# The bias of a projection copied into its PSUM banks one item earlier

## The chip, the cores and the metric

The kernel runs on one core of one Trainium2 chip. The metric is the device time of the whole kernel in microseconds (us); smaller is better. A core has five engines that run side by side and meet through semaphores: TensorE (PE in the profile, its weight loads PEld), VectorE (DVE), ScalarE (ACT), GpSimd (POOL) and SyncE (SP), which here only issues DMA transfers. Matmuls write to PSUM[...]; ACT and DVE read them from there.

## The reference

Two graph layers with a residual and a layer norm each, on x of 16 batches x 1024 nodes x 128 features and one 1024 x 1024 matrix `adj`, all in float32:

```python
# layer 0
support = einsum('bnf,fo->bno', x, weight)
x = layernorm(x + einsum('nm,bmo->bno', adj, support) + bias)
# layer 1: five steps of a gated unit, h = x at the start
m  = einsum('nm,bmd->bnd', adj, h);  av = concat([m, m])
u3 = h @ u3_w.T + u3_b
z  = sigmoid(av @ w3_w.T + w3_b + u3);  r = sigmoid(av @ w4_w.T + w4_b + u3)
hv = tanh(av @ w5_w.T + w5_b + (r * h) @ u5_w.T + u5_b)
h  = (1 - z) * h + z * hv
x = layernorm(x + h)
```

The kernel multiplies by `adj` first and by `weight` after it, which gives the same sum for layer 0.

## The kernel before

Batches are taken four at a time (a quad; `q` counts four of them). For each quad, `aggregate` multiplies `adj` by the four batches. It doesn't do this block by block: it uses a scheme of seven products in place of eight, on two levels. On the outer level there are seven products, done in four groups, each by one call of `chain`: the groups are named 12, 3, 67 and 54. On the inner level, each chain has seven items again, taken in the order 1, 5, 6, 2, 7, 3, 4. An item is a set of matmuls (L398) into one of three PSUM banks: pa for items 1 and 2, pc for 5 and 3, pb for 6, 7 and 4. In chain 12, 67 and 54 an item has four matmuls of 256 columns, in chain 3 two. The profile lists two records for each float32 matmul.

Behind each item stands one reading of its bank: ACT copies (L382 from pa into pb after item 1, L383 after 5, L384 after 6, L385 after 2, L388 after 4) and DVE additions (L386 after 7, L387 after 3). The next item that uses the bank has to wait for that reading. So item 4 of a chain can write pb only after L386 has read item 7 there.

DVE forms the sums that the scheme needs on the way in (L317 to L320 for the inner level, L347 to L351 for the outer), and the sums on the way out (L437, L446 to L448, L455, L457), which fill the tile `agg` with the four aggregated batches.

Layer 0 is done for all four quads first, in the aggregations with the tags x0 to x3. The rest of layer 0 for the quad before, the projection, is put inside the next aggregation: `projections` (L664) hands `chain` 12 a dictionary of hooks, functions to be called ahead of an item. Batch k of the quad is projected ahead of item 5 (k = 0), 2 (k = 1), 3 (k = 2) and at the end of chain 12 (k = 3). The last quad's projections lie in the first aggregation of layer 1, tag 0_0. So there are four blocks with four projections each: in x1, x2, x3 and 0_0.

A projection (`project`) works in two PSUM banks, seeded0 and seeded1, one for each half of the 1024 nodes. For each half ACT copies the bias, broadcast to 512 columns, into the bank (L469); four chunks are added to it by matmuls of 128 columns with the weight (L472, eight matmuls or sixteen records for both halves); DVE adds the bank to the input (L477). Since there is one pair of banks, the copy of a projection must wait until L477 of the projection before has read them. Then follow the statistics of the layer norm on DVE (L256, L258), its scale and shift on POOL (L269 to L272), and its application on ACT (L275), which `drain` puts one or two at a time behind later items; at last a DMA stores the batch (L281).

Later, in layer 1, the same two banks serve the gates (L506, L531); the change doesn't touch that part.

What sets the order of instructions: the framework orders each engine's instructions by dependencies and priorities. `tc.keep_in_program_order` keeps marked instructions of an engine in the order of the code, `tc.high_priority` draws instructions ahead where they can go. The readings behind the items, the bias copies and L477 have high priority, so their places among others follow from the framework's plan, and so do the places of the matmuls between them. An engine executes its own list in order. In the compiled order of before, projection 0 lies behind the third of the four products of item 5, projection 1 behind the third of item 2, projection 2 between items 7 and 3, and projection 3 inside chain 3, between the two products of its item 5.

Of the kernel before, what the change touches and what calls it, by code (L numbers as in the profile page):

```python
# [20 lines left out]
def kernel(  # L21
# [32 lines left out]
    nc = tc.nc  # L54
    B, N, D = x.shape
    P = 128
# [4 lines left out]
    CH = C // 2  # L61
# [10 lines left out]
    rows = const.tile([P, QUAD, N], F32, name="rows")  # L72
# [16 lines left out]
    seeded = [ps_m.tile([P, HALF], F32, name=f"seeded{i}") for i in range(2)]  # L89
# [14 lines left out]
    def chunked(t):  # L104
        return t.rearrange("p (c d) -> p c d", c=C)

    def chunk_cols(t, c):

        return t.rearrange("p (n q c) -> p n c q", n=4, c=2)[:, c // 2, c % 2]
# [5 lines left out]
    def x_rows(b):  # L115
        return x[b].rearrange("(p c) d -> p (c d)", c=C)
# [10 lines left out]
    for i, c in enumerate([*range(CH), "x0", "x1", *range(CH, C), "x2", "x3"]):  # L127
        queue = queues[i % 2 if i < 6 else 0]
        if isinstance(c, str):
            k = int(c[1])  # L130
# [77 lines left out]
    b0_bc = const.tile([P, D], F32, name="b0_bc")  # L208
# [6 lines left out]
    def layer0_weights():  # L215
        nc.sync.dma_start(w0_sb, w0)
        nc.sync.dma_start(b0_bc, bass.AP(tensor=b0.tensor, offset=b0.offset, ap=[[0, P], [1, D]]))
# [114 lines left out]
    def sums_of(src, ns, pinned=False):  # L332
        t = inner[0 if ns in ((1, 2), (6, 7)) else 1]
        for op in inner_sums(blocks_of(src, ns), [t[:, i, : len(ns)] for i in range(4)]):
            if pinned:
                tc.keep_in_program_order(op)
        return op
# [16 lines left out]
    def behind_closing():  # L354

        return tc.issue_after(closed[0].ins) if closed[0] else nullcontext()
# [100 lines left out]
                nc.vector.tensor_add(agg[:, dst, :HALF], agg[:, dst, :HALF], p5[:, cols])  # L457


    def project(q, k, y):  # L460

        b = q * QUAD + k
        y = chunked(y)
        for h in range(2):
            po = seeded[h]
            po3 = po.rearrange("p (k d) -> p k d", k=CH)
            with tc.high_priority():
                tc.keep_in_program_order(
                    nc.scalar.copy(po3, b0_bc[:, None, :].broadcast_to([P, CH, D]))  # L469
                )  # L470
            for c in range(CH):
                nc.tensor.matmul(  # L472
                    po3[:, c, :], chunk_cols(agg[:, k], h * CH + c), w0_sb, start=False, stop=True,
                    skip_group_check=True,
                )
            with tc.high_priority():
                nc.vector.tensor_add(y[:, ts(h, CH), :], po3, y[:, ts(h, CH), :])  # L477
        layernorm(y, f"0_{b}", chunked(saved[b]))
# [175 lines left out]
    def call(f, *args):  # L654
        return lambda: f(*args)


    def projections(q):

        room = rooms[q % 2]  # L660
        ys = [ypad[0], ypad[1], room[:, 2], room[:, 3]]
        for k in (2, 3):
            nc.sync.dma_start(ys[k], x_rows(q * QUAD + k))
        return {a: [call(project, q, k, ys[k])] for k, a in enumerate((5, 2, 3, "end"))}  # L664

    def added_left():

# [41 lines left out]
    for q in range(NQ):  # L709
        room = rooms[q % 2]  # L710
        hooks = {}
        if q == 0:
            hooks[12] = {
                5: [turn_rest, added_sums, added_left],
                6: [outer_left, call(sums_of, rows, (3,))],
                7: [rest_sums, call(inner_left, 6), call(inner_left, 7)],
            }
            hooks[67] = {1: [call(inner_left, 5), call(inner_left, 4)]}
            layer0_weights()
            with tc.issue_after(last_left.ins):  # L720
                sums_of(rows, (1, 2))
        else:
            hooks[12] = projections(q - 1)
            hooks[12][6] = [call(sums_of, room, (3,)), call(outer_sums, room, False, True)]

        def fetch(q=q):
            drain(99, 0)
            if q == 0:

                for dst, b in [(hid[:, k], QUAD + k) for k in range(QUAD)] + [  # L730
                    (ypad[k], k) for k in range(2)
                ]:
                    tc.keep_in_program_order(nc.gpsimd.dma_start(dst, x_rows(b)))
                load_layer1_weights()
                return
            for k in range(2):
                nc.sync.dma_start(ypad[k], x_rows(q * QUAD + k))
            if q + 1 < NQ:
                load(q + 1, rooms[(q + 1) % 2], x_rows)
            else:  # L740
                load(0, rows, saved_rows)

        def ahead(room):
            sums_of(room, (1, 2))
            outer_sums(room, True, False)

        hooks.setdefault(67, {})["end"] = [fetch]
        hooks[54] = {7: [call(ahead, rooms[(q + 1) % 2])]}
        if q == 1:
            hooks[54][5] = [layer1_weights]  # L750
            hooks[54][4] = [turn_weights]
        if q == 0:
            with tc.issue_after(last_left.ins):
                aggregate(f"x{q}", room, hooks, False)
        else:
            aggregate(f"x{q}", room, hooks, False)
# [83 lines left out]
    for q in range(NQ):  # L840
        for s in range(STEPS):
            tag = f"{q}_{s}"
            if s == 0:
                if q == 0:
                    hooks = {
                        12: projections(NQ - 1),
                        3: {5: [call(to_hidden, 0)], 2: [call(to_hidden, 1)]},
                        67: {
                            3: [call(drain, 99, 0), call(to_hidden, 2)],
                            "end": [call(to_hidden, 3)],  # L850
                        },
                        54: {},
                    }
                    hooks[12][6] = [call(sums_of, rows, (3,)), call(outer_sums, rows, False, True)]
                else:
                    outer_sums(rows)
                    hooks = {54: {}}
            else:
                hooks = {54: {}}
            last = s == STEPS - 1  # L860
            end = last and q == NQ - 1

            k = s if q else s - 1
            if q < NQ - 1 and 0 <= k < QUAD:
                hooks[3] = {1: [call(next_load, q + 1, k)]}
                hooks[67] = {1: [call(next_turn, k)]}
            if q > 0 and s > 0:
                hooks.setdefault(67, {})[5] = [call(close_load, q - 1, s - 1)]
                hooks[54] = {6: [call(close, q - 1, s - 1)]}
            if q == s == 0:  # L870
                hooks[54][3, (0,)] = [call(gates_begin, tag, 3)]
            hooks[54][4] = [call(gate_r, 0, False)]
            hooks[54][3, (1,)] = [call(gate_z, 0)]
            aggregate(tag, rows, hooks, s > 0)
            if end:
                load(q, rows, saved_rows)
            elif last:
                load(q + 1, rows, saved_rows)
            with behind_closing():
                gate_rh(0)  # L880
            if not end:
                gate_seed(2)
            gate_r(1)
            gate_z(1)
            if end:
                turns[0] = part_of[2]
                ending(q, tag)
                break

            def updated(k):  # L890
                if last:
                    turn_rows(k, None, closing[k])
                    fetch_hidden(k)
                elif k < 3:
                    turn_rows(k)
                    if k < 2:
                        fetch_rows(k)

            def step_update(u, part):
                k, h = UNITS[u]  # L900
                if last and u == 4:
                    sums_of(rows, (1, 2))
                    sums_of(rows, (3,))
                update_half(tag, k, h, part, not last and k == 3)
                if u % 2:
                    updated(k)

            for u in range(3, 8):
                gate_first(tag, u, (u - 3) % 3)
                step_update(u - 3, (u - 2) % 3)  # L910
                gate_r(u - 1)
                gate_z(u - 1)
            step_update(5, 2)
            gate_r(7)
            gate_z(7)
            step_update(6, 0)
            step_update(7, 1)
            part_of.insert(0, part_of.pop())
            then = f"{q}_{s + 1}" if not last else f"{q + 1}_0"
            gates_begin(then, 2 if q == NQ - 1 and s == STEPS - 2 else 3)  # L920
            if not last:
                fetch_rows(3, 1)
                fetch_rows(3, 0)
# [32 lines left out]
```

## Time and profile before

| | us |
|---|---|
| three runs | 1771.13, 1771.18, 1771.88 |
| their median | 1771.18 |
| span of the profiled execution, first to last instruction | 1769.3 |
| PE busy in it | 1757.7 (99%) |
| DVE busy | 1302.9 (74%) |
| ACT busy | 799.2 (45%) |
| POOL busy | 103.6 (6%) |
| the four blocks in it, start of the first projected item to the last projection | 61.4 to 79.1, 112.4 to 130.1, 163.0 to 180.7, 213.7 to 231.4 |
| 32 bias copies L469 on ACT | 17.8, 0.595 each |
| 32 additions L477 on DVE | 21.5, 0.69 each |

The profile is of one execution; the page gives its span, and no device time for it. In the lists by order of time a row has its start, its length, engine, line, operation, what it writes and reads, its size, and how many instructions were drawn together (x). In brackets stands how long the engine was idle before it and what ended this. Lengths include some time in which the next instruction of the engine already runs, so the step from start to start is the better measure. The clock that TensorE was granted is 0.999 over the whole span.

### The profile page before, as it was taken

The numbers are of one execution on the slowest core, as the hardware profiler recorded it, in microseconds if no ns is written. First come the engines' busy times: TensorE is split into PE (matmuls) and PEld (weight loads), VectorE is DVE, ScalarE is ACT, GpSimd is POOL, SyncE is SP. The second block draws the span as 40 slices with busy tenths as digits, with TensorE's granted clock in tenths as the row PEclk, the third lists the DMA queues.
The fourth block names the chain that finished last, engine by engine and source line by source line (L and its number), as shares of the span: only waits on it lengthen the run. The fifth ranks groups of instructions, "written<-read, shape, count | busy, mean of one in ns | idle before, by whom it ended". The sixth has DMA issues, their size and how long they took to land.

```text
span 1769.3 us, 19948 instructions
## 1 busy us (share of the span) xinstructions
PE 1757.7 (99%) x6709; PEld 1264.5 (71%) x6709; DVE 1302.9 (74%) x2286; ACT 799.2 (45%) x1424; POOL 103.6 (6%) x152
## 2 busy tenths in 40 slices
PE   9999999999999999999999999999999999999997
PEld 8888885766758577685867758586675857668584
DVE  7977777676766857777777667777778577777778
ACT  4355555344352434435354442535445353443537
POOL 1202120000000000000000000000000000000004
PEclk9999999999999999999999999999999999999999
DMA  8144354141422505143351424324243241514232
GB/s 276 49 143 143 120 130 107 26 114 30 96 60 72 143 13 130 48 121 68 87 131 54 114 54 101 81 75 119 53 114 98 58 92 28 131 25 107 60 84 95
DMA packets 405332, 161.34 MB, mean 91 GB/s; under 512 B 388336, under 2 KB 389488, under 8 KB 405232
## 3 DMA queue, kind: packets, MB, share of 16 engines
q1 hardware_dynamic: 402960, 153.01, 34.1%
q0 software_dynamic: 1696, 5.24, 1.1%
q10 hardware_dynamic: 576, 1.84, 0.3%
q8 instruction: 53, 0.87, 0.2%
q14 instruction: 47, 0.39, 0.1%
HBM read 93.98 MB, written 65.01 MB: 90 GB/s over the span
## 4 chain that ended last, share of the span: by engine, by line
PE 98%; DMA 1%; DVE 0%; POOL 0%; ACT 0%; issue 0%; POOLq 0%; SPq 0%; DVEq 0%; ACTq 0%
PE pb L398 25%; PE pc L398 14%; PE pa L398 14%; PE pu L516 8%; PE ph L539 8%; PE ph L540 8%; PE pu L498 8%; PE seeded L531 8%; PE pc_x L398 3%; PE pa_x L398 3%; PE seeded L472 2%; DMA hid<-in_adj_dram 1%; DMA agg<-in_adj_dram 0%; PE pt L630 0%; PE pt_end L831 0%; POOL rstd L265 0%
## 5 line engine op out<-in xcount | busy, mean ns | idle before, releaser
L398 PE MATMUL pb<-e,inner 128*128 128x256 f32 x864 | 206.3, 379 | 0.2 <-ACT pb L382 0.2
L555 DVE TENSOR_TENSOR tsum<-tsum,hid 128x512 f32<-128x512 f32 x158 | 108.7, 688 | 106.4 <-ACT tsum L550 106.3
L550 ACT ACTIVATE tsum<-ph,bh 128x512 f32<-128x512 f32 x158 | 108.6, 687 | 164.3 <-PE ph L540 164.2
L398 PEld LDWEIGHTS pb<-e,inner 128*128 128x128 f32 x864 | 167.7, 194 | 19.5 <-ACT pb L382 0.9
L516 PE MATMUL pu<-agg,w_t 128*128 128x512 f32 x320 | 163.7, 593 | 0.0
L539 PE MATMUL ph<-agg,w_t 128*128 128x512 f32 x320 | 163.4, 592 | 0.0
L531 PE MATMUL seeded<-agg,w_t 128*128 128x512 f32 x320 | 163.4, 592 | 0.0
L540 PE MATMUL ph<-tsum,u_t 128*128 128x512 f32 x320 | 163.4, 592 | 0.0
L498 PE MATMUL pu<-hid,u_t 128*128 128x512 f32 x320 | 157.0, 592 | 0.0
L519 ACT ACTIVATE tsum<-pu,br 128x512 f32<-128x512 f32 x160 | 110.1, 688 | 85.5 <-PE pu L516 85.5
L398 PE MATMUL pb<-s,inner 128*128 128x256 f32 x576 | 148.4, 380 | 0.0
L398 PE MATMUL pb<-a,inner 128*128 128x256 f32 x576 | 143.9, 379 | 0.0
L526 DVE TENSOR_TENSOR tsum<-tsum,hid 128x512 f32<-128x512 f32 x160 | 110.2, 688 | 37.7 <-ACT tsum L519 37.7
L398 PE MATMUL pc<-e,inner 128*128 128x256 f32 x560 | 134.3, 379 | 0.0
L398 PEld LDWEIGHTS pb<-s,inner 128*128 128x128 f32 x576 | 110.5, 194 | 24.6 <-issue 10.2
L534 ACT ACTIVATE tsum<-seeded,bz 128x512 f32<-128x512 f32 x160 | 110.0, 688 | 29.3 <-PE seeded L531 29.3
L398 PEld LDWEIGHTS pb<-a,inner 128*128 128x128 f32 x576 | 111.9, 194 | 12.4
L398 PEld LDWEIGHTS pc<-e,inner 128*128 128x128 f32 x560 | 109.1, 195 | 12.7 <-issue 0.7
L540 PEld LDWEIGHTS ph<-tsum,u_t 128*128 128x128 f32 x320 | 60.8, 190 | 76.5 <-issue 59.1
L539 PEld LDWEIGHTS ph<-agg,w_t 128*128 128x128 f32 x320 | 60.6, 190 | 75.1 <-issue 74.4
L498 PEld LDWEIGHTS pu<-hid,u_t 128*128 128x128 f32 x320 | 60.8, 190 | 73.5 <-issue 72.2
L556 DVE TENSOR_TENSOR tsum<-tsum 128x512 f32<-128x512 f32 x158 | 109.1, 691 | 4.9
(192 smaller groups left out, 2856.3 us busy)
## 6 DMA issues: line engine op xcount, KB each, us to landing
turned<-ypad SPq DMA_DIRECT2D x48, 512.0 KB, 3.8
rows<-turned SPq DMA_DIRECT2D x192, 128.0 KB, 2.8
hvs<-saved SPq DMA_DIRECT2D x24, 512.0 KB, 4.1
rows<-saved SPq DMA_DIRECT2D x20, 512.0 KB, 3.8
hid<-hidden SPq DMA_DIRECT2D x64, 128.0 KB, 3.3
turned<-ypad SPq DMA_DIRECT2D x32, 256.0 KB, 2.9
rows<-turned SPq DMA_DIRECT2D x128, 64.0 KB, 2.1
hidden<-ypad SPq DMA_DIRECT2D x12, 512.0 KB, 4.1
```

What stands on the lines that cost most here:

```text
L398: product = nc.tensor.matmul(bank_of[a][:, ts(o, QT)], chunk(a, o, c), left[n][a][:, c, :], start=(a in (1, 5) and o == 0 and c == 0), sto ...
L498: in_order(nc.tensor.matmul(pu, w_t["u3"], hid[:, k, ts(h, HALF)], start=True, stop=True, skip_group_check=True))
L516: in_order(nc.tensor.matmul(pu, w_t["w4"], agg[:, k, cols], start=False, stop=True, skip_group_check=True))
L519: pin(nc.scalar.activation(rh[:, cols], pu, AF.Sigmoid, bias=br))
L526: pin(nc.vector.tensor_mul(rh[:, cols], rh[:, cols], hid[:, k, cols]))
L531: in_order(nc.tensor.matmul(pz, w_t["w3"], agg[:, k, cols], start=False, stop=True, skip_group_check=True))
L534: pin(nc.scalar.activation(z_of[k % 2][:, cols], pz, AF.Sigmoid, bias=bz))
L539: in_order(nc.tensor.matmul(ph, w_t["w5"], agg[:, k, cols], start=True, stop=False))
L540: in_order(nc.tensor.matmul(ph, w_t["u5"], rh_of[k % 2][:, cols], start=False, stop=True))
L550: pin(nc.scalar.activation(hv, ph, AF.Tanh, bias=bh))
L555: pinned(nc.vector.tensor_sub(hv, hv, hid[:, k, cols]))
L556: pinned(nc.vector.tensor_mul(hv, hv, z_of[k % 2][:, cols]))
```

## The change

The copies of the bias leave `project` and become a function of their own, `seed_bias`, which writes both banks. It is called by hooks one item earlier: ahead of item 1 for the projection ahead of item 5, ahead of 6 for the one ahead of 2, ahead of 7 for the one ahead of 3, and ahead of 4 for the one at the end. Where item 6 has hooks of its own, the lists are joined, with the copies first.

```diff
+    def seed_bias():
+        for po in seeded:
+            with tc.high_priority():
+                tc.keep_in_program_order(nc.scalar.copy(
+                    po.rearrange("p (k d) -> p k d", k=CH),
+                    b0_bc[:, None, :].broadcast_to([P, CH, D]),
+                ))
+
     def project(q, k, y):
...
         for h in range(2):
-            po = seeded[h]
-            po3 = po.rearrange("p (k d) -> p k d", k=CH)
-            with tc.high_priority():
-                tc.keep_in_program_order(
-                    nc.scalar.copy(po3, b0_bc[:, None, :].broadcast_to([P, CH, D]))
-                )
+            po3 = seeded[h].rearrange("p (k d) -> p k d", k=CH)
             for c in range(CH):
                 nc.tensor.matmul(
...
-        return {a: [call(project, q, k, ys[k])] for k, a in enumerate((5, 2, 3, "end"))}
+        hooks = {a: [call(project, q, k, ys[k])] for k, a in enumerate((5, 2, 3, "end"))}
+        hooks.update({a: [seed_bias] for a in (1, 6, 7, 4)})
+        return hooks
...
-            hooks[12][6] = [call(sums_of, room, (3,)), call(outer_sums, room, False, True)]
+            hooks[12][6] += [call(sums_of, room, (3,)), call(outer_sums, room, False, True)]
...
-                    hooks[12][6] = [call(sums_of, rows, (3,)), call(outer_sums, rows, False, True)]
+                    hooks[12][6] += [call(sums_of, rows, (3,)), call(outer_sums, rows, False, True)]
```

The compiled order follows suit. On ACT the copies of projection 0 come ahead of L382, those of projection 1 ahead of L384, those of projection 2 stay behind L385, those of projection 3 come ahead of L388. On TensorE each projection stands whole between two items: 0 behind item 1, 1 behind item 6, 2 behind item 7, 3 behind item 4 and ahead of chain 3. On DVE the additions L477 come some places earlier among the statistics and sums. The lists of POOL and SP are the same.

## Prediction

> **What bounds the kernel now.** I read the page first, then the view of the instructions on the projection's line L472, then TensorE's order of time around one block, then the busy time of the four blocks, and last the rows of VectorE and of TensorE's weight loads behind each block.
>
> ```profile
> span 1769.3 us, 19948 instructions
> PE 1757.7 (99%) x6709; PEld 1264.5 (71%) x6709; DVE 1302.9 (74%) x2286; ACT 799.2 (45%) x1424; POOL 103.6 (6%) x152
> PE 98%; DMA 1%; DVE 0%; POOL 0%; ACT 0%; issue 0%; POOLq 0%; SPq 0%; DVEq 0%; ACTq 0%
> ```
> ```profile
> L472 PE MATMUL seeded<-w_sb,agg x256: 272/281/386, 62.8 to 233.3; 128*128 128x128 f32 x128
> ACT seeded L469: 3.5, 12
> ```
> TensorE sets the end. The bias copies L469 hold its weight loads back 12 times, 3.5 us in all. There are 16 projections, so four don't wait.
>
> ```profile
> 61.41 1.56 PE L398 MATMUL pc_x<-e,inner 128*128 128x256 f32 x6
> 62.81 2.13 PE L472 MATMUL seeded<-w_sb,agg 128*128 128x128 f32 x16
> 64.78 0.60 PE L398 MATMUL pc_x<-e,inner 128*128 128x256 f32 x2
> 65.21 1.89 PE L398 MATMUL pb<-e,inner 128*128 128x256 f32 x8
> 66.94 1.46 PE L398 MATMUL pa_x<-a,hid 128*128 128x256 f32 x6
> 68.32 2.15 PE L472 MATMUL seeded<-w_sb,agg 128*128 128x128 f32 x16
> 70.31 0.60 PE L398 MATMUL pa_x<-a,hid 128*128 128x256 f32 x2
> 70.75 1.89 PE L398 MATMUL pb<-e,inner 128*128 128x256 f32 x8
> 72.47 2.04 PE L472 MATMUL seeded<-w_sb,agg 128*128 128x128 f32 x16
> 74.35 1.89 PE L398 MATMUL pc_x<-e,hid 128*128 128x256 f32 x8
> ```
> Read the starts, not the lengths: rows overlap. Eight 256-column records take 1.73 us (65.21 to 66.94), and sixteen of a projection that doesn't wait take 1.88 (72.47 to 74.35).
>
> ```profile
> 61.41:79.14 17.73, 17.73 (x104) 15.67 (x103) 17.21 (x64) 6.51 (x13) 6.43 (x8) 1.00 0.29 90
> 112.37:130.09 17.72, 17.72 (x103) 15.66 (x103) 17.38 (x49) 6.50 (x13) 2.46 (x4) 1.00 0.30 100
> ```
> Here PE, PEld, DVE, ACT and POOL follow the length. ACT is busy 6.5 us of 17.7; VectorE 97 to 98%. It is the second limit in these blocks, and it already shows behind them, where item 4 of chain 3 may write bank pb only after L386 has read it:
>
> ```profile
> 135.37 0.42 DVE L386 TENSOR_TENSOR agg<-pb,agg 128x256 f32<-128x256 f32 x1
> ...
> 186.10 0.41 DVE L386 TENSOR_TENSOR agg<-pb,agg 128x256 f32<-128x256 f32 x1
> ...
> 236.89 0.41 DVE L386 TENSOR_TENSOR agg<-pb,agg 128x256 f32<-128x256 f32 x1
> ```
> ```profile
> 186.56 0.73 PEld L398 LDWEIGHTS pb<-s,inner 128*128 128x128 f32 x4 [0.22 <-DVE agg L386]
> ...
> 237.35 0.73 PEld L398 LDWEIGHTS pb<-s,inner 128*128 128x128 f32 x4 [0.32 <-DVE agg L386]
> ```
>
> **What the Trainium skill says.** "Perfetto Trace Analysis", Tensor Engine Instruction: a matmul's reported end is computed, not observed. The overlapping rows agree, so I use starts. "TensorE: Matmul & The Clock Gate", Step-by-step: weight loads may be pulled ahead of running matmuls. The load of the projection at 72.47 starts at 72.26, so some 0.1 to 0.2 us of a load's wait is hidden. The same page, Architectural detail: ScalarE and VectorE are strictly first in, first out. So a copy that waits holds the queue behind it; no row contradicts it. "PSUM — Partial Sum Buffer", PSUM bank collisions: two engines must not touch one bank and quadrant at once. That is why a bias copy must wait for L477's read of its bank; no run here shows a collision.
>
> **The change part by part.**
>
> *Removed: the wait.* In block x1, projection 0 is late by 1.40 - 6 x 0.216 = 0.10 before it and 1.97 - 1.88 = 0.09 inside; projection 1 by 1.38 - 1.29 = 0.09 and 1.99 - 1.88 = 0.11; projection 2 by nothing; projection 3 (79.14 to 81.12, after two records from 78.67) by 0.04 and 0.10. Sum 0.53. The starts of x2, x3 and 0_0 give 0.53 to 0.55. Four blocks: 2.15 us, which is the most that the change can free.
>
> *Added: nothing.* 32 copies of 0.595 us (17.8 us) stay on ACT, and every instruction stays. POOL's and SP's queues keep their orders, so no DMA is moved past another.
>
> *Moved on ACT.* In the compiled order the copies pass L382 (projection 0), L384 (1) and L388 (3); those of 2 stay behind L385. Let T be the start of projection 0, the end of item 1. With no wait TensorE runs projection 0 at T, 1 at T+5.34, 2 at T+10.68, 3 at T+16.02, each after two items of 1.73. The copies of 0 follow the previous L388 (59.44 in x1) and end near 61.1, before T = 61.4. Those of 1 follow L383 behind item 5, as those of 2 followed L385 before: 70.94 + 0.49 + 0.59 = 72.02, ahead of the load at 72.26, which had no wait. So they cost nothing if the bank is free in time.
>
> *The new condition: L477 of the projection before.* Behind a waiting copy stand L384, L385 or L388, whose banks are written again at least one item later. When the reads end I work out from VectorE's compiled order with the pitches of the rows of before (0.60 for an L477, 1.15 for an L347, L348 or L350, 0.26 for a pair of statistics), each L477 starting no sooner than 0.2 us after its matmuls. Projection 0: in x1 the first half's matmuls end at T+0.94, VectorE comes from L455 and L457 at T+1.66, so the two reads end by T+2.9; in x2 L347 stands ahead of them with its DMA wait of 0.34, so T+3.9. Wanted: the item-5 copy L383 starts at T+3.8, the bias copies follow 0.49 later, so T+4.3 for the first bank and T+4.8 for the second. Projection 1: in x1 its reads stand behind the statistics and L350 and end at T+7.3 and T+9.2; in x2 and x3 at T+8.3 or sooner; wanted T+9.6 and T+10.2. Projection 2: reads end near T+13.5 in all; with 1.3 for both copies that is T+14.8, against T+16.0. So no copy is late and I take nothing. The cover is 0.4 to 1.2 us; if it is gone, each such copy costs its excess. Bounds 0 and 0.2 us for each of the 12 projections behind another.
>
> *Moved on TensorE.* Projections 0 and 1 come three products earlier, 3 goes from inside chain 3 to ahead of it. Projection 0 then needs agg of batch 0: the first half is done long before, the second by L455 at 61.27 + 0.69 = 61.96, wanted at T + 0.94 = 62.35. Nothing. The second half now waits for two engines; a semaphore instruction on this queue took 51 ns once, so 0 to 0.2 us for four. I take 0.
>
> *Moved on VectorE: the gain meets L386.* Its work ahead of L386 is the same; only its idle time can shrink. TensorE comes 0.54 sooner to item 4 of chain 3. VectorE's idle in the blocks is 0.33 + about 0.1 (x1), 0.29 (x2), 0.15 + 0.18 (x3), 0.27 + 0.18 (0_0). With L477 earlier most of it goes, but the second L477 of projection 3 comes to the head of VectorE up to 0.15 us before its matmuls end. So L386 comes earlier by about 0.42, 0.27, 0.25, 0.30. In x1 item 4 starts at 85.44, L386 ends at 85.02: the slack holds and 0.53 stays. In x2 the load (135.85) follows L386's end (135.79) already, with 0.13 of wait hidden; 0.27 more costs about 0.26, so 0.28 stays. In x3 a wait of 0.22 cost TensorE 0.09; 0.29 more leaves 0.26. In 0_0 0.32 cost 0.19; 0.24 more leaves 0.30. Sum 0.53 + 0.28 + 0.26 + 0.30 = 1.4 us. What is late next in the three blocks is L386. Bounds 0.5 (VectorE gains nothing in those three) and 2.15.
>
> Behind L386 there is room: the first sum for chain 67 ends at 188.1, wanted at 189.04. All later orders are equal, so the gain is carried to the end.
>
> **Sum.** The profiled span of 1769.3 becomes 1767.9. The page gives no device time of its own for that execution; the runs' median of 1771.18 lies 1.9 above the span, which stays. 1771.18 - 1.4 = 1769.8.
>
> **Rivals.** *All of it stays:* VectorE loses its idle time and more, since L477 is spread among small rows. For it: x1 has slack. Against: 97 to 98% busy. 1771.18 - 2.15 = 1769.0. *Nearly all is given back at L386* in x2, x3 and 0_0; only x1 gains: 1770.6. For it: VectorE's idle there was never over 0.45. *Slower:* L477 now stands early in VectorE's order, and with a first-in, first-out queue each one that reaches the head before its matmuls are done idles the engine that is nearly full, and L386 comes later than before. It decides from where new idle exceeds the old (0.29 to 0.45 a block, and 0.53 more over the three to eat x1's gain). At 0.75 new idle in each of the three: 3 x (0.75 - 0.36) - 0.53 = +0.6, 1771.8. Against: by the rows of before, only one L477 a block comes early, by 0.15. That the copies don't move at all is excluded by the compiled order.
>
> **Chances.** Forecast 0.53, all stays 0.21, given back 0.15, slower 0.11. The range leaves out most of the slower case and adds the runs' scatter (0.75 us) at the ends: 1768.6 to 1771.4. A change of 0.2% (3.5 us) is about what a measurement of this kernel can tell from none; the most to be gained is 2.15 us. So same 0.94, faster 0.03, slower 0.03.
>
> **What would show it.** Right: no wait of the projections for the bias copy, each projection 1.88 from start to start, blocks shorter by some 0.5 us to the end of projection 3, and in x2, x3 and 0_0 a longer wait for L386 at item 4 of chain 3. Wrong: copies that wait for L477 beyond an item's end, a TensorE wait at a projection, L386 late by over 0.7 us, or a difference behind 240 us.

## The result, and the profile after

| | before | after |
|---|---|---|
| median of 21 runs each, same chip, us | 1771.38 (1770.95 to 1771.88) | 1768.44 (1768.08 to 1769.02) |
| span of the profiled execution | 1769.3 | 1766.9 |
| last matmul's start to the end of the span | 9.26 | 8.83 |

The ratio is 0.9983, with a 95% interval of 0.9977 to 0.9990: 2.9 us less. The interval leaves out 1: 2.9 us are told from nothing here, where the prediction took about 3.5 us for the least that can be. The forecast was 1.4 us less; the time lies 0.16 us below the lower end of its range.

The page of after, its span, busy times and chain:

```profile
span 1766.9 us, 19951 instructions
PE 1755.7 (99%) x6709; PEld 1265.8 (72%) x6709; DVE 1301.9 (74%) x2286; ACT 800.0 (45%) x1424; POOL 103.3 (6%) x152
PE 98%; DMA 1%; DVE 0%; POOL 0%; ACT 0%; issue 0%; POOLq 0%; SPq 0%; DVEq 0%; ACTq 0%
```

TensorE is still the bound. Lines below the new function have moved by three: the copies are L463, the projections' matmuls L475, their reads L480 (L477 before). The view of L475:

```profile
L475 PE MATMUL seeded<-w_sb,agg x256: 272/281/282, 61.6 to 230.2; 128*128 128x128 f32 x128
L475 PEldq EVENT_SEMAPHORE  x5: 51/51/51, 57.7 to 211.5; - x5
its engine sat idle before it (us, times) until:
who waited for it (us, times):
```

The list of waits is empty where before it had twelve waits for ACT, and the longest record is 282 ns instead of 386. The four more semaphore instructions are the second engine that a projection now waits for. The view of the copies L463 shows where waiting went:

```profile
L463 ACT COPY seeded<-b_bc x32: 589/593/597, 60.1 to 226.0; 128x512 f32<-128x512 f32 x32
its engine sat idle before it (us, times) until:
  DVE hid L480: 5.4, 3
  DVE rows L480: 4.4, 4
who waited for it (us, times):
```

The copies wait 9.8 us for VectorE's reads, in seven places, all of them at projection 3, and nobody waits for the copies: ACT has the time. TensorE's order of time in x1:

```profile
61.60 2.04 PE L475 MATMUL seeded<-w_sb,agg 128*128 128x128 f32 x16
63.48 1.89 PE L398 MATMUL pc_x<-e,inner 128*128 128x256 f32 x8
65.21 1.89 PE L398 MATMUL pb<-e,inner 128*128 128x256 f32 x8
66.93 2.04 PE L475 MATMUL seeded<-w_sb,agg 128*128 128x128 f32 x16
68.81 1.89 PE L398 MATMUL pa_x<-a,hid 128*128 128x256 f32 x8
...
77.59 2.04 PE L475 MATMUL seeded<-w_sb,agg 128*128 128x128 f32 x16
79.47 1.03 PE L398 MATMUL pa_x<-s,hid 128*128 128x256 f32 x4
```

Every projection takes 1.88 us from start to start and every item 1.73, as forecast: from 61.60 to 79.47 nothing is left to gain. Behind the blocks, item 4 of chain 3 waits for L386 in x2, x3 and 0_0; weight loads of after:

```profile
135.18 0.73 PEld L398 LDWEIGHTS pb<-s,inner 128*128 128x128 f32 x4 [0.36 <-DVE agg L386]
...
185.39 0.73 PEld L398 LDWEIGHTS pb<-s,inner 128*128 128x128 f32 x4 [0.28 <-DVE agg L386]
...
235.53 0.73 PEld L398 LDWEIGHTS pb<-s,inner 128*128 128x128 f32 x4 [0.22 <-DVE agg L386]
```

That is the forecast give-back, but smaller: in x3 0.28 against 0.22 before, in 0_0 0.22 against 0.32. Only x2, which had none, has a clear new wait.

**Where the 2.4 us of the two spans went.** I compare the start of the same matmul record in both traces. The first projected block begins 0.20 later in after. The blocks then gain 0.56 (x1), 0.32 (x2), 0.49 (x3) and 0.65 (0_0), together 2.02. At 696 us, in a part that the change does not touch, 0.19 more is gained. The rest behind the last matmul is 0.43 shorter. 0.20 - 2.02 - 0.19 - 0.43 = -2.44, and the spans, 1769.31 and 1766.88, differ by 2.43. The 0.20 at the start is scatter: in the other traces of this study this point lies between -0.14 and +0.51 of that of before, and before alone has 0.51 between its two traces. Over all runs the median span is 1766.5 after; before it is 1769.2 to 1769.3 in the three sets of runs beside the experiments (1769.7 in the 13 runs of before_again). That is 2.7 to 2.8, of which 2.6 are the three gains named.

So two things are to be explained: why the blocks kept 2.0 of 2.15 us and not 1.4, and where 0.6 us outside the blocks came from.

### The profile page after: what moved, and what is told of

It is laid out like the page before. It is cut to its first block, busy times and chain, and to the rows that moved or that the text cites. A ratio compares the mean times of both kernels' runs of the same rounds, so it can differ in the third digit from the quotient of the medians.

```text
span 1766.9 us, 19951 instructions
## 1 busy us (share of the span) xinstructions
PE 1755.7 (99%) x6709; PEld 1265.8 (72%) x6709; DVE 1301.9 (74%) x2286; ACT 800.0 (45%) x1424; POOL 103.3 (6%) x152
## 4 chain that ended last, share of the span: by engine, by line
PE 98%; DMA 1%; DVE 0%; POOL 0%; ACT 0%; issue 0%; POOLq 0%; SPq 0%; DVEq 0%; ACTq 0%
PE pb L398 25%; PE pc L398 14%; PE pa L398 14%; PE pu L519 8%; PE ph L542 8%; PE pu L501 8%; PE ph L543 8%; PE seeded L534 8%; PE pc_x L398 3%; PE pa_x L398 3%; PE seeded L475 2%; DMA hid<-in_adj_dram 1%; DMA agg<-in_adj_dram 0%; PE pt L633 0%; PE pt_end L836 0%; POOL rstd L265 0%
```

## Experiments

**Both kernels again**, unedited.

> The kernel before once more, for a second profile and for what two equal programs differ by: 0.0 within 0.3 us. The twelve waits at the projections return (3.5 us of weight loads, 0.53 us of TensorE a block). If the stall near 696 us and the longer time behind the last matmul belong to this program, they return too; if they are scatter, they don't.

> The changed kernel once more, for a second profile. If the gain beyond the four blocks (the first profile has 2.0 us in the blocks, 0.2 lost at the start, 0.2 gained near 696 us, 0.4 gained behind the last matmul) is scatter of single executions, those parts come out differently here and the blocks give 2.0 again; the median stays 2.9 us below before. If they belong to the change, the same parts return within 0.1.

Measured: 1771.47 (1770.95 to 1772.02) and 1768.45 (1768.07 to 1769.57); ratios to the runs of before beside them 1.0001 (0.9993 to 1.0009) and 0.9985 (0.9978 to 0.9991). The medians of before_again and of the runs of before beside it are 0.30 us apart: so far do equal programs differ. In the two traces the blocks of after again gain 0.56, 0.45, 0.49 and 0.65 = 2.14 over the first trace of before; the stall at 696 us is in both traces of before and in neither of after; the rest behind the last matmul is 9.23 against 8.79. So the parts outside the blocks belong to the kernels, and are not scatter.

**Less work on VectorE, in both kernels.** Layer 0's layer norm takes every second chunk's statistics only, and applies each to two chunks:

```diff
+        every = 2 if tag.startswith("0_") else 1
+        n //= every
...
-                pin(nc.vector.bn_stats(stats[:, c, :], y[:, c, :]))
+                pin(nc.vector.bn_stats(stats[:, c, :], y[:, every * c, :]))
...
```

> The kernel before with the same half of the layer norm's statistics left out. If the twelve waits for the copies alone make the difference, it keeps them and is slower than the changed kernel with half of the statistics by the whole 2.15 us of the four blocks; VectorE's relief alone takes away the waits for L386 in x3 and 0_0, 0.1 to 0.3 us. If relieving VectorE brought the copies forward too, the waits at the projections would shrink.

> The changed kernel, but the layer norm of layer 0 takes statistics of every second chunk only (each is applied to two chunks), which takes 16 x 8 small instructions, about 1.0 us a projection, off VectorE. If VectorE's late L386 gives part of the gain back, its waits of 0.36, 0.28 and 0.22 us in x2, x3 and 0_0 go, and the kernel is about 0.4 to 0.5 us faster than the changed one (1768.0). If VectorE plays no part, it is the same as the changed one within 0.2 us.

Measured: 1771.31 (1771.10 to 1771.73), ratio 1.0001 (0.9992 to 1.0009); and 1769.34 (1768.52 to 1769.92), ratio 0.9989 (0.9982 to 0.9996). The second is 0.9 us slower than after, though it does less; 1768.0 had been expected. In before_half_stats the twelve waits for the copies stay, 3.5 us as before, so relief of VectorE alone does not bring the copies forward. In x3 and 0_0 the waits for L386 are gone from both kernels: before_half_stats gains 0.09 and 0.17 over before there, and the change is worth 0.55 and 0.56 (trace against trace of the pair), which is all of the 0.53. But the framework's plan used the room otherwise. In x2 it put a sum ahead of the reading (VectorE of after_half_stats; the reading is L389 in it):

```profile
133.90 1.22 DVE L440 TENSOR_TENSOR agg<-first 128x1024 f32<-128x1024 f32 x1
135.04 0.41 DVE L389 TENSOR_TENSOR agg<-pb,agg 128x256 f32<-128x256 f32 x1
```

The weight load then waits 0.52 us, and x2 gains only 0.17. And behind 0_0 both kernels of the pair have a new wait, of the first matmul of a gate for a sum into `agg` (TensorE of after_half_stats):

```profile
265.16 1.10 PE L522 MATMUL pu<-agg,w_t 128*128 128x512 f32 x2 [0.37 <-DVE agg L458]
```

It costs 0.61 from start to start in both. So x3 and 0_0, where item 4 stands directly behind item 3 as in after, show that VectorE's late L386 is what holds those blocks back; the times of the whole kernels mix in two new waits.

**Projection 3 later in the code**, ahead of item 5 of chain 3, so that VectorE reads item 7 of chain 3 ahead of many of its statistics:

```diff
-        hooks = {a: [call(project, q, k, ys[k])] for k, a in enumerate((5, 2, 3, "end"))}
+        hooks = {a: [call(project, q, k, ys[k])] for k, a in enumerate((5, 2, 3))}
...
-        return hooks
+        return hooks, {5: [call(project, q, 3, ys[3])]}
...
-            hooks[12] = projections(q - 1)
+            hooks[12], hooks[3] = projections(q - 1)
...
```

> The changed kernel, but projection 3 is emitted ahead of item 5 of chain 3 in place of the end of chain 12, so that VectorE reads item 7 of chain 3 (L386) ahead of many of projection 3's statistics. If what is left of the waits at item 4 of chain 3 (0.36, 0.28 and 0.22 us of the weight load in x2, x3 and 0_0) is VectorE being late with L386, these waits go and the blocks gain their full 0.53 each: some 0.3 to 0.5 us less than the changed kernel, 1768.0. Rival: the statistics put off make something later late (the first sum for chain 67, or a bias copy that waits for L477), and the time is 1768.4 or more.

Measured: 1768.27 (1768.01 to 1768.89), ratio 0.9983 (0.9976 to 0.9990). Weight loads of late3 around item 4 of chain 3 (`pb<-s,inner`), in x2, and item 4 alone in x1:

```profile
133.85 0.84 PEld L398 LDWEIGHTS pc_x<-e,rows 128*128 128x128 f32 x4
134.71 0.41 PEld L398 LDWEIGHTS pa_x<-s,tsum 128*128 128x128 f32 x2
135.14 0.84 PEld L398 LDWEIGHTS pb<-s,inner 128*128 128x128 f32 x4
136.00 0.41 PEld L398 LDWEIGHTS pa_x<-s,tsum 128*128 128x128 f32 x2
...
84.41 0.73 PEld L398 LDWEIGHTS pb<-s,inner 128*128 128x128 f32 x4 [0.27 <-DVE agg L386]
```

No bracket in x2, nor in x3 and 0_0: all three waits for L386 are gone, those that before had too. But an earlier reading is not what removed them. L386 starts 0.56, 0.65 and 0.65 us behind the start of item 3 (the end of item 7) there, in after 0.53, 0.44 and 0.38: statistics went behind it, and the plan put sums (of L317 to L319) ahead of it in their place. What changed is TensorE's order. Two loads of the next chain's first item (`pa_x<-s,tsum`) now stand ahead of item 4, so that it needs its bank 0.43 to 0.48 us later; in after, item 4 of these blocks follows item 3 directly. In x1 it is the other way round: there before and after have the two loads, late3 has not, and a new wait of 0.27 stands in their place.

The blocks gain 0.42, 0.55, 0.64 and 0.76 = 2.37 over before, 0.2 to 0.35 more than after. So the run shows what the three blocks gain when TensorE need not wait for L386, the 0.53 and in x3 and 0_0 what that wait had cost before; it does not show that an earlier reading brings it. The two medians differ by 0.17, in the right direction; against the scatter of the runs that is not shown to be a gain.

What L386 costs TensorE can be read from the starts. From the last record ahead of item 4 to the first behind it are 1.08 us where nothing waits. What is above that is in all four blocks together 0.26 in before, and 0.46, 0.33 and 0.23 in the three traces of after's order (after, after_again, and after_four_more_act below). So L386 takes back 0.2 us of the change at most, where the forecast had 0.75.

**Copies early, matmuls at their old places.** The projections' matmuls are held inside the items, where before has them:

```diff
+                    inside = hooks.get(("mid", a), ()) if (o, c) == (len(ns) - 1, 1) else ()
+                    for hook in inside:
+                        hook()
...
+        at = (("mid", 5), ("mid", 2), 3)
+        hooks = {a: [call(project, q, k, ys[k])] for k, a in enumerate(at)}
...
```

> The bias copies early as in the changed kernel, but the projections' matmuls held at the places that they have in the kernel before, inside the items. TensorE's waits for the bias go as in the changed kernel (2.15 us). Theory that VectorE lost its stalls because its additions L477 now lie among rows where their matmuls are long done: here L477 comes with before's timing, so the stalls of VectorE stay near before's 1.05 us per block, against 0.45 in the changed kernel. L386 stands early in VectorE's order here, so that does not cost TensorE: 1768.3 to 1769.0. Rival, that the stalls go because TensorE is earlier, wherever the matmuls stand: the stalls fall to about 0.45 here too.

Measured: 1769.41 (1768.75 to 1770.14), ratio 0.9990 (0.9983 to 0.9996). The blocks gain 0.44, 0.43, 0.60 and 0.64 = 2.12, like after, and then 0.61 is lost behind 0_0 to the same wait of a gate's first matmul for `agg` (0.37 in brackets) as in the pair above. VectorE's stalls are 0.56, 0.65, 0.53 and 0.49 us per block. The theory, that it is the new places of L477 that free VectorE, falls: at the old places the stalls are nearly halved as well (before has 1.02 to 1.09; the table below says how they are counted). The rival holds: they shrink because TensorE comes earlier. The plan moved item 4 of chain 3 behind two loads of the next chain in x2, x3 and 0_0 here too, as in late3, so the gains of this run's blocks do not tell what L386 costs.

**One part at a time.** First only the copies of projections 0 and 1 early, then only those of 3:

```diff
-    def project(q, k, y):
+    def project(q, k, y, own=False):
...
             po3 = seeded[h].rearrange("p (k d) -> p k d", k=CH)
+            if own:
+                with tc.high_priority():
+                    tc.keep_in_program_order(
+                        nc.scalar.copy(po3, b0_bc[:, None, :].broadcast_to([P, CH, D]))
+                    )
...
-        hooks = {a: [call(project, q, k, ys[k])] for k, a in enumerate((5, 2, 3, "end"))}
-        hooks.update({a: [seed_bias] for a in (1, 6, 7, 4)})
+        hooks = {a: [call(project, q, k, ys[k], k > 1)] for k, a in enumerate((5, 2, 3, "end"))}
+        hooks.update({a: [seed_bias] for a in (1, 6)})
```

The second has `k < 3` in place of `k > 1` and `(4,)` in place of `(1, 6)`.

> Only the copies of projections 0 and 1 come one item early; those of 2 and 3 stay inside the projection. TensorE is freed of 0.19 + 0.20 us in each block, 1.55 in all. Theory that VectorE has 1.02 to 1.09 us of stalls per block before, most of them L477 waiting for the matmuls of these two projections, which TensorE's wait passes on: VectorE wins back nearly what TensorE wins, L386 takes back little, and the blocks gain 1.3 to 1.55 us; with the 0.6 outside the blocks, if it comes, 1769.3 to 1769.4, without it 1769.9. Rival, that VectorE's idle time is the 0.29 to 0.45 of its bracketed rows, as the prediction has it: x2, x3 and 0_0 keep about half, the blocks gain 0.9 to 1.0, and the time is 1770.3 (1769.7 with the 0.6).

> Only the copies of projection 3 come one item early. TensorE is freed of 0.14 us in each block, 0.56 in all, but projection 3 comes directly ahead of chain 3 and its wait for L386, and the stalls of VectorE ahead of it stay. Theory: x1 keeps 0.14, in x2, x3 and 0_0 L386 takes most of it back, so the blocks gain 0.15 to 0.35 us: 1771.0, and 0.6 less if the parts outside the blocks come. Rival, that L386 comes earlier by as much as TensorE: 0.56, 1770.7.

Measured: 1769.18 (1768.91 to 1770.11), ratio 0.9989 (0.9982 to 0.9995); and 1770.57 (1770.15 to 1771.37), ratio 0.9996 (0.9988 to 1.0005), which alone is not told from no change. The waits that are left, in the view of the projections' matmuls of early_0_and_1_only:

```profile
its engine sat idle before it (us, times) until:
  ACT seeded L477: 1.1, 4
```

and of early_3_only:

```profile
its engine sat idle before it (us, times) until:
  ACT seeded L477: 2.4, 8
```

(L477 is the copy here.) Together they are the 3.5 us and 12 times of before: each part removes its own waits and no others. The blocks gain 0.41, 0.40, 0.35 and 0.50 = 1.67 with the first part, and 0.15, 0.15, 0.15 and 0.14 = 0.59 with the second. The theory for projection 3, that L386 takes most of it back, falls; the rival, that L386 comes earlier by as much as TensorE, holds: against the starts of x2, x3 and 0_0 it comes 0.14 to 0.15 us earlier with the second part. VectorE's stalls tell why:

| kernel | TensorE freed per block | VectorE's stalls in x1, x2, x3, 0_0 (us) |
|---|---|---|
| before | | 1.05, 1.03, 1.02, 1.09 |
| early_3_only | 0.14 | 0.86, 0.87, 0.88, 0.95 |
| early_0_and_1_only | 0.39 | 0.62, 0.71, 0.67, 0.62 |
| after | 0.53 | 0.43, 0.85, 0.47, 0.47 |

A stall is the time from the start of a row to the start of the next, less the usual step of such a row (0.60 for an L477, 0.18 for a statistic, 0.09 for its aggregate); those of 0.05 and more are added up from the start of a block to L386 of chain 3. On the mean of the four blocks they shrink by 0.16 and 0.39 in the two parts, and in after by 0.6 apart from x2. That is about what TensorE was freed of.

**Four more instructions on ScalarE, five more on VectorE.** After the change ScalarE executes four records fewer and VectorE five more, semaphore instructions among them. Each count is undone or imitated at the very start, with every later order unchanged:

```diff
-    nc.scalar.copy(warm, power[:, :1])
+    for _ in range(5):
+        nc.scalar.copy(warm, power[:, :1])
```

in after, and in before

```diff
-    nc.vector.memset(power, -0.5)
+    for _ in range(6):
+        nc.vector.memset(power, -0.5)
```

> The changed kernel with four more copies of one column on ScalarE at the very start, which no engine waits for. Theory that the 0.2 us at 696 us and the 0.4 us behind the last matmul come from the places at which instruction transfers fall, and that ScalarE's number of instructions (four fewer in the changed kernel) sets them: both come back, 1769.0, with a tail of 9.2 us behind the last matmul and the weight loads' wait of 0.31 at 696. Rival, that ScalarE's count is not what sets them: no change, 1768.4, tail 8.8.

> The kernel before with five more fills of a small tile on VectorE at the very start, so that VectorE's instructions number as in the changed kernel. Theory that VectorE's position in its instruction transfers sets the 0.2 us at 696 us and the 0.4 us of the tail: both go, 1770.8. Rival: no change, 1771.4.

Measured: 1768.55 (1768.19 to 1770.39), ratio 0.9986 (0.9979 to 0.9992); and 1771.11 (1770.60 to 1771.58), ratio 0.9999 (0.9991 to 1.0007). The medians alone say nothing at this size; the traces do. ScalarE's copy behind item 1 of a chain, at the same place of the program, in before, after and after_four_more_act:

```profile
696.20 0.36 ACT L382 COPY pb<-pa 128x256 f32<-128x256 f32 x1 [0.61 <-PE pa L398]
```
```profile
694.10 0.36 ACT L382 COPY pb<-pa 128x256 f32<-128x256 f32 x1 [0.33 <-PE pa L398]
```
```profile
693.84 0.36 ACT L383 COPY pb<-pa 128x256 f32<-128x256 f32 x1 [0.61 <-PE pa L399]
```

(The added line moves L382 to L383.) With ScalarE's count restored the copy is late by 0.28 us again, and TensorE loses its 0.19. VectorE's count does not touch it (0.61 in before_five_more_dve). The last outputs, in the DMA list over the last 10 us, of before and of before_five_more_dve (KB each, median us from issue to landing):

```profile
out_dram<-rows SPq DMA_DIRECT2D x2, 128.0 KB, 2.5
out_dram<-rows ACTq DMA_DIRECT2D x1, 256.0 KB, 2.9
```
```profile
out_dram<-rows SPq DMA_DIRECT2D x2, 128.0 KB, 2.0
out_dram<-rows ACTq DMA_DIRECT2D x1, 256.0 KB, 2.4
```

With five more instructions on VectorE the outputs land 0.5 us sooner, and the rest behind the last matmul is 8.81 us in place of 9.26 (median span 1768.9 against 1769.3). ScalarE's count does not touch that (8.79 in after_four_more_act). So each of the two parts comes from the number of one engine's instructions ahead of it. The theory had given both parts to either engine; it is one each.

What carries the count is likely the transfer of instructions. "Runtime: NRT & Kernel Launch", Instruction fetch mechanics, of the Trainium skill says that each sequencer fetches its instructions in blocks of 16 KiB by a DMA queue of its own while it executes, at a cost that is mostly hidden. This kernel's page lists 53 instruction packets of 16 KB and 47 of 8 KB, so not every block here has the size that the skill gives. The counts fit such transfers: 13,793 records of TensorE and its weight loads over 53 packets are 260 each, and the 6,155 of the other four engines over 47 are 131 each, half as many in packets half as large. Those of 8 KB stand at the two places, where something is not hidden. Their starts, shifted to the time of before:

| kernel | a transfer near 697 | idle of L382 there | a transfer in the rest | rest behind the last matmul |
|---|---|---|---|---|
| before, before_again | 696.9 | 0.61 | 1765.2 | 9.26, 9.23 |
| early_3_only | 698.8 | 0.33 | 1765.2 | 9.24 |
| after, after_again | 698.8 | 0.33 | 1763.9, 1764.2 | 8.83, 8.79 |
| after_four_more_act | 696.9 | 0.61 | 1764.0 | 8.79 |
| before_five_more_dve | 696.9 | 0.61 | 1763.9 | 8.81 |
| early_0_and_1_only | 696.8 | 0.61 | 1764.1 | 8.79 |

In these eight traces, and in the other four likewise, the stall and the long rest go with the place of the transfer without exception. At 1765.2 it falls among the pieces of the last outputs, at 1764 ahead of the last of them. That the transfer itself causes the delay is inferred from this; the count of instructions is shown.

## Why the prediction was wrong

**The removed wait was right.** 0.53 us per block, 2.15 in all: after it, the projections have no wait, and the two parts alone give the 0.39 and 0.14 that the starts had shown for them.

**The copies cost nothing, as said.** Seven of them wait for the read of the projection before, 9.8 us in all, and nobody waits for them. (They would have to wait without the rule on PSUM banks that the prediction gave as the reason: they overwrite what is read.) Projection 0's need of `agg` and the four semaphore instructions cost nothing that the starts show.

**The step that failed first: "only its idle time can shrink", with the idle time read as 0.29 to 0.45 us a block.** That was the sum of the brackets (in x2 without its wait for a DMA, 0.34). The stalls from start to start were 1.02 to 1.09. Here are rows of VectorE around the reads of projections 1 and 3 in x3 of before:

```profile
170.78 0.26 DVE L256 BATCH_NORM_STATS2 stats<-ypad 128x6 f32<-128x128 f32 x1
171.19 0.69 DVE L477 TENSOR_TENSOR ypad<-seeded,ypad 128x512 f32<-128x512 f32 x1 [0.15 <-issue]
171.80 0.24 DVE L258 BATCH_NORM_AGGREGATE mv<-stats 128x2 f32<-128x6 f32 x2
172.15 0.69 DVE L477 TENSOR_TENSOR ypad<-seeded,ypad 128x512 f32<-128x512 f32 x1
...
181.67 0.26 DVE L256 BATCH_NORM_STATS2 stats<-rows 128x6 f32<-128x128 f32 x1
182.00 0.69 DVE L477 TENSOR_TENSOR rows<-seeded,rows 128x512 f32<-128x512 f32 x1
182.61 0.17 DVE L258 BATCH_NORM_AGGREGATE mv<-stats 128x2 f32<-128x6 f32 x1
182.96 0.69 DVE L477 TENSOR_TENSOR rows<-seeded,rows 128x512 f32<-128x512 f32 x1 [0.18 <-PE seeded L472]
```

From 170.78 to 171.19 are 0.41 us where a statistic takes 0.18: a stall of 0.23, of which the bracket shows 0.15. From 171.80 two aggregates should take 0.18, and L477 starts after 0.35: 0.17, and no bracket at all. At 182.00 it is 0.15 without a bracket, at 182.96 0.26 with a bracket of 0.18. Two more, of 0.11 and 0.09, have none either; the sum is 1.02 in a block whose brackets give 0.33. Part of the rest is idle time under 0.15 us, for which no view here prints a bracket (0.11 ahead of 172.15, 0.07 ahead of 182.00); the rows' lengths cover the other part. "Perfetto Trace Analysis", DVE / Act Engine Instruction, of the Trainium skill says why they can: such a row runs until the write is acknowledged, while the next instruction may begin before. This trace agrees, with 0.69 of length and 0.60 to 0.61 of step for an L477. The prediction itself warned to read the starts and not the lengths, used starts for TensorE, and then took lengths for VectorE; the 97 to 98% of busy time was of the same kind. The same rows in after:

```profile
168.88 0.67 DVE L480 TENSOR_TENSOR ypad<-seeded,ypad 128x512 f32<-128x512 f32 x1
169.47 0.17 DVE L258 BATCH_NORM_AGGREGATE mv<-stats 128x2 f32<-128x6 f32 x1
169.55 0.26 DVE L256 BATCH_NORM_STATS2 stats<-ypad 128x6 f32<-128x128 f32 x1
169.77 0.69 DVE L480 TENSOR_TENSOR ypad<-seeded,ypad 128x512 f32<-128x512 f32 x1
```

The reads of projection 1 come 2.3 us sooner, 1.6 against the start of the block, with no more than 0.04 of stall. No such addition starts, in any trace, sooner than 0.25 us behind the last matmul whose sum it reads. In before 18 of the 32 start 0.26 to 0.27 behind it, so these had waited for it; in after it is 12, in copies_early_old_places 11. Most of what VectorE lost before was waiting for matmuls which themselves waited for the bias: TensorE's wait was passed on to it. Take the wait away, and both come earlier by about as much.

**What followed from it.** L386 was to come earlier by 0.27, 0.25 and 0.30 us in x2, x3 and 0_0; against the starts of the blocks it came earlier by 0.28, 0.49 and 0.65. So x3 kept 0.49 where 0.26 was forecast, and 0_0 0.65 where 0.30 was: it kept more than its 0.53, since the older wait for L386 shrank too. x1 kept 0.56 (0.53). The mechanism, L386 as the next late thing, was right: TensorE waits for it in three blocks of after, and where VectorE has less to do, in x3 and 0_0 of the pair above, the whole 0.53 stays. What these two blocks keep was put at half of what it became, since VectorE's idle time was. This is 0.6 us of the error.

**x2 was right by luck.** It kept 0.32 where 0.28 was forecast, but its stalls did not shrink as in the others. VectorE there waits for a DMA; in before, after, after_again and after_four_more_act:

```profile
113.86 1.22 DVE L347 TENSOR_TENSOR tsum<-rows 128x1024 f32<-128x1024 f32 x1 [0.34 <-DMA rows<-in_x_dram]
```
```profile
113.92 1.23 DVE L347 TENSOR_TENSOR tsum<-rows 128x1024 f32<-128x1024 f32 x1 [0.77 <-DMA rows<-in_x_dram]
```
```profile
113.47 1.23 DVE L347 TENSOR_TENSOR tsum<-rows 128x1024 f32<-128x1024 f32 x1 [0.63 <-DMA rows<-in_x_dram]
```
```profile
113.31 1.23 DVE L348 TENSOR_TENSOR tsum<-rows 128x1024 f32<-128x1024 f32 x1 [0.45 <-DMA rows<-in_x_dram]
```

The block begins 0.36 earlier in after, the data does not come earlier: by the starts the stall grows from 0.43 to 0.85. Then the 0.6 us of stalls at L477 and L386 vanish, and the block still gains. The last three traces have the same order on each engine, apart from four copies at the start of the last. Their stalls here are 0.85, 0.71 and 0.53, their waits for L386 0.36, 0.24 and none, and x2 gains 0.32, 0.45 and 0.55. So what x2 gives back goes with the landing of a transfer. The prediction knew this wait, but its idle time for x2, 0.29, is the bracket of an L477; that the DMA's wait would grow by what the block gains was none of its terms.

**The step that failed second: "All later orders are equal, so the gain is carried to the end."** The orders are equal, and the gain was carried, but equal orders did not mean equal times: 0.19 us at 696 and 0.4 behind the last matmul came on top, set by the number of instructions on ScalarE and on VectorE. It was no part of any case, though the prediction named a difference behind 240 us as a sign of being wrong. Nor was 2.15 the most that the change could free: the blocks gain 2.24 in after_four_more_act and 2.37 in late3, since before had itself lost 0.26 to L386. Without the part outside the blocks the time would have been about 1769.1, inside the range.

**The rivals.** "All of it stays", 1769.0, came nearest: the blocks gained 2.02, 2.14 and 2.24 in the three traces of after's order, against 2.15. Its reason, that VectorE loses its idle time and more, was the right one; that the reads stand among small rows was not needed for it. "Given back" and "slower" are excluded: VectorE's stalls fell in every block.

**The sum again.** Forecast -1.4; L386 -0.6; outside the blocks -0.6: -2.6, of the 2.7 to 2.8 us by which the median spans differ and the 2.9 of the medians. The remaining 0.2 to 0.3 is no more than the scatter ahead of the first block and in x2; where it lies stays open.

## What to carry to other kernels

When one engine's wait holds up a second engine's input, the second engine's stalls are part of the same wait: both shrink together, unless the second engine waits for something else as well, as in x2 for a DMA. So price the give-back from what the second engine waits for, and not from how busy it is. Measure stalls of short instructions from start to start against the usual step of such a row; brackets show less than half of them here (1.7 us of brackets, 2.4 us with the short gaps that have none, for 4.2 us of stalls in the four blocks). When a run takes a wait away, look at how: in late3 the order of the waiting engine had changed, and not the time of what it waits for. Where gains of 0.1% are forecast, the range needs half a microsecond for what a changed number of instructions does in places that the change doesn't touch.

## What the hardware showed that was not expected

- Five tiny fills at the start of the kernel (0.07 us each) shortened the rest behind the last matmul, 1760 us later, from 9.26 to 8.81 us; four tiny copies on ScalarE brought a stall of 0.28 us back at 694 us.
- A weight load's wait of 0.2 to 0.4 us for L386 costs TensorE 0.1 to 0.2 us: 0.36, 0.28 and 0.22 cost 0.23, 0.15 and 0.08 in after.
